# Maxima of three causal attentions: masking the diagonal blocks in SBUF in place of with products

## The chip, the cores and the metric

The kernel runs on one core of one Trainium2 chip. The core has TensorE (PE in the profile: matrix products, results go to the accumulation memory PSUM), VectorE (DVE), ScalarE (ACT), GpSimd (POOL) and SyncE (SP, which here issues DMAs). Each engine takes its own instructions in the order in which they were written; between engines, instructions wait for semaphores. The metric is the device time of one execution in microseconds, smaller is better.

## The reference

A post-norm decoder of two layers on x of 8 batches, 256 tokens and 512 features: in the first layer a differential attention with grouped heads, a long convolution against a context, and a mixture of eight experts with two chosen for each token; in the second a self attention, a cross attention against the context, and an attention with keys and values routed to one head of sixteen. After each of the six, `x = layernorm(x + f(x))`. Three of the six are causal attentions of the form

```
scores = einsum("bhqd,bhkd->bhqk", q, k) * scale
scores = where(causal, scores, very_negative)     # key later than query: hidden
probs  = softmax(scores)                          # exp(score - max over the visible keys), divided by its sum
out    = einsum("bhqk,bhkd->bhqd", probs, v)
```

The softmax subtracts for each query the maximum of its visible scores. This maximum is what the change is about.

## The kernel before

The six parts run one after the other. The three causal attentions share one function, `causal_attention` (L1109): the first runs from about 20 to 470 us of the span, the second from about 1203 to 1541, the third from about 1941 to 2265. Between them stand the convolution and the experts (to 1203) and the cross attention (1541 to 1941).

A **unit** is one batch and four heads. The first attention has 8 units for each of 8 batches, 64 in all (it has 32 heads of scores); the second and third have 4 for each batch, 32 each. Units are numbered `u`; `upb` is the number for each batch. In each unit the 256 tokens make two blocks of 128 queries and two of 128 keys, and since keys later than the query are hidden, three score blocks count: (first queries, first keys) and (second, second), which lie on the diagonal and are half hidden, and (second, first), which is visible as a whole.

What a unit does is spread over `upb + 1` units of the loop (L1357):

- `maxima(u)` (L1154): scores with queries on the partitions. TensorE writes for four heads `s` the three blocks `j` into `ps_q`, a PSUM tile of four banks, one bank for each head. First come four products of `ident_b` and `hide_b` (L1161), which write 0 for visible and -1e30 for hidden pairs into both diagonal blocks; then 12 score products (L1171), each in a 32-row strip of the array, which add to them. VectorE takes the negated maxima of all three blocks with one reduction (L1178) into `neg`.
- After the last unit of a batch, `split(n)` (L1186) joins the two blocks of the second queries and splits the maxima into three bf16 terms (seven small VectorE instructions, L1189 to L1196), and `turn(n)` (L1199) transposes them on TensorE (L1204) and ScalarE copies them out as `negT` (L1212).
- `weights(u)` (L1214), one batch later: scores again, now with keys on the partitions (L1225), with the maxima added by small products (L1234), into `ps_k`; then ScalarE's exp into `pT` (L1242), GpSimd's select that zeroes the hidden half of the diagonal blocks (L1243), and, save in the last batch, a GpSimd add (L1253) that joins two blocks for the row sums.
- `products(u)` (L1255), one unit after that, called by `sums` (L1345): values (L1268), which need the select, and row sums by a matrix of ones (L1278), which need the add, into the PSUM tile `ps_pv`; VectorE's reciprocal of the sums (L1286) and the product with it (L1292, in the first attention L390 and, for the second of a pair of heads, L393 with a GpSimd add L394).

`ps_q` and `ps_k` share one buffer: `maxima(u)` can't begin before the exp of the weights before it, and the weights of a unit can't begin before its maxima are read. `ps_pv` has one buffer too; three more, of the tag `mm`, are for everything else.

The engines' order within the attentions is the order in which the code is written (`manual_schedule`). The loop writes, for each unit: `maxima`, at a batch's end `split`, `sums`, then "mid" events, a short portion of **fill**, `weights`, at a batch's end `turn`, the rest of the fill, "end" events. Fill is other TensorE work cut into steps: projections for the next group of tokens (L205), transposes (L217), output products of finished batches (L205), with its readers on ScalarE or VectorE. When an output tile is complete, VectorE adds the residual (L234) and takes mean and variance (L168, L169), GpSimd computes the reciprocal root (L163, L164), and VectorE normalises one unit later (L177). These GpSimd instructions are written where the fill ended, so they can stand ahead of the unit's select L1243. The first attention also has a GpSimd power for each finished tile of a batch (L469), written as an "end" event.

Of the kernel before, what the change touches and what calls it, by code (L numbers as in the profile page):

```python
# [16 lines left out]
F32 = mybir.dt.float32  # L17
BF16 = mybir.dt.bfloat16
AF = mybir.ActivationFunctionType
ALU = mybir.AluOpType  # L20
AX = mybir.AxisListType
PSUM = bass.MemoryType.PSUM

P = 128
# [7 lines left out]
FAR = 1.0e30  # L32
# [17 lines left out]
def decoder_kernel(ctx: ExitStack, tc: tile.TileContext, a: dict, out: bass.AP):  # L50
    nc = tc.nc
# [4 lines left out]
    const = ctx.enter_context(tc.tile_pool(name="const", bufs=1))  # L56
# [10 lines left out]
    def load_x(tiles):  # L67
# [8 lines left out]
    ident_b = const.tile([P, P], BF16, tag="ident_b", name="ident_b")  # L76
    nc.vector.tensor_copy(ident_b, ident)
    hide_b = const.tile([P, P], BF16, tag="hide_b", name="hide_b")
    nc.gpsimd.memset(hide_b, 0.0)
    nc.gpsimd.affine_select(  # L80
        out=hide_b,
        in_=hide_b,
        compare_op=ALU.is_ge,
        fill=-FAR,
        base=0,
        pattern=[[-1, P]],
        channel_multiplier=1,
    )

# [3 lines left out]
    nc.gpsimd.memset(ones_v, 1.0)  # L93

    mask = const.tile([P, 2 * P], F32, tag="mask", name="mask")
    nc.gpsimd.memset(mask, 0.0)
    nc.gpsimd.affine_select(
        out=mask[:, P:],
        in_=mask[:, P:],
        compare_op=ALU.is_ge,  # L100
        fill=FAR,
        base=0,
        pattern=[[-1, P]],
        channel_multiplier=1,
    )
    neg_half = const.tile([P, H1], F32, tag="neg_half", name="neg_half")
# [1002 lines left out]
    def causal_attention(name, prepare, finish, upb=KB, gather=None):  # L1109
# [9 lines left out]


        engines = {
            mybir.EngineType.PE,
# [4 lines left out]
        with ExitStack() as st:  # L1127
# [26 lines left out]
            def maxima(u):  # L1154
                g, b, c = unit(u)
                q, k, _ = groups[g]
                ps = ps_sc.tile([P, 4, D], F32, tag="sc", name="ps_q")
                block = ps[:, :, : 3 * P].rearrange("p s (j k) -> p s j k", j=3)

                for s in range(4):  # L1160
                    nc.tensor.matmul(  # L1161
                        block[:, s, 0:3:2, :],
                        lhsT=ident_b,
                        rhs=hide_b.unsqueeze(1).broadcast_to([P, 2, P]),
                        start=True,
                        stop=False,
                    )
                for j, (i, keys) in enumerate(((0, 0), (1, 0), (1, 1))):
                    for s in range(4):
                        rows = slice(32 * s, 32 * s + 32)  # L1170
                        nc.tensor.matmul(  # L1171
                            block[:, s, j, :],
                            lhsT=q(rows, c, b * S + i * P, P),
                            rhs=k(rows, c, b * S + keys * P, P),
                            start=False,
                            stop=(j == 2),
                        )
                nc.vector.tensor_reduce(  # L1178
                    neg[(u // upb) % 2][:, :, :, c].rearrange("p j s -> p s j"),
                    block,  # L1180
                    AX.X,
                    ALU.max,
                    negate=True,
                )
# [171 lines left out]
            left = 0.0  # L1356
            for u in range(units + lag + 2):  # L1357
# [6 lines left out]
                if u >= units:  # L1364
# [7 lines left out]
                    continue  # L1372
                maxima(u)
                if u % upb == upb - 1:
                    split(u // upb)
                sums(u)
                happen("mid")
# [6 lines left out]
                if u >= upb:  # L1384
                    weights(u - upb)
                if u % upb == upb - 1:
                    turn(u // upb)
                left = fill(left + rate - short)
                happen("end")
# [464 lines left out]
```

## Time and profile before

| | |
|---|---|
| median of 3 runs | 2280.09 us (2278.44 to 2285.2) |
| the profiled execution's own time | 2277.43 us |
| its span, from first to last instruction | 2275.7 us |
| granted TensorE clock, mean | 0.971 of full speed |
| TensorE busy | 2110.2 us |
| VectorE busy | 1245.9 us |
| GpSimd busy | 679.2 us |
| ScalarE busy | 415.9 us |
| window 83 to 473 us (first attention): PE, DVE, ACT, POOL busy | 355.5, 248.0, 116.3, 190.7 of 390 us |
| window 1203 to 1541 us (second) | 327.9, 178.6, 78.8, 105.6 of 338 us |
| window 1941 to 2265 us (third) | 308.1, 219.5, 66.3, 80.8 of 324 us |

In the lines of a profile "L1178" is a line of the kernel, "neg<-ps_q" what is written and read, "x128" how many. In the groups of part 5 the numbers after the bar are the busy time in us, the mean of one in ns, and the idle time of the engine just before them with what ended most of it. In a timeline the columns are start and duration in us, engine, line, operation, operands and how many are merged; square brackets give the idle time of that engine before it and what released it. In the list of waits they are the total in us, the number of times and the longest. PE is busy time of pipelined products, so its share says little of how close it is to its peak. "PEld" is the loading of weights, which overlaps.

### The profile page before, as it was taken

How to read it: one execution, taken by the hardware profiler on the slowest of the kernel's cores; microseconds unless marked ns; L12 is line 12 of the kernel's file. 1: busy time of each engine (PE TensorE's matmuls, PEld its weight loads, DVE VectorE, ACT ScalarE, POOL GpSimd, SP SyncE). 2: the span in 40 equal slices, each digit the busy share in tenths (PEclk: the TensorE clock that was granted, in tenths of full speed). 3: DMA queues.
4: the chain of work that ended last, by engine and by line, in shares of the span. 5: the costliest groups of instructions: out<-in, count | busy, mean ns of one | idle time of the engine just before them, and what ended most of it. 6: DMA issues, size and time to landing. Idle time of an engine off the chain costs nothing. (4 is left out here: it accounts for less than half of the span.)

```text
span 2275.7 us, 36145 instructions
## 1 busy us (share of the span) xinstructions
PE 2110.2 (93%) x15416; PEld 1236.4 (54%) x15416; DVE 1245.9 (55%) x1923; ACT 415.9 (18%) x595; POOL 679.2 (30%) x780
## 2 busy tenths in 40 slices
PE   7799989888999997999969999997999999999996
PEld 4455555544445455555534454555877875555543
DVE  3566666666889874122234556456343332566767
ACT  1223233330001002211111222221101101122212
POOL 0345544555555833000021334224000000022323
PEclk9899999998999999999989999999999999999998
DMA  7899702403313225123140102002000000000000
GB/s 236 303 384 384 267 2 66 115 1 109 136 44 136 80 92 181 61 81 119 56 158 19 47 29 75 1 1 94 29 19 28 28 10 1 1 11 10 15 15 29
DMA packets 110032, 197.60 MB, mean 87 GB/s; under 512 B 7088, under 2 KB 30768, under 8 KB 109872
## 3 DMA queue, kind: packets, MB, share of 16 engines
q1 hardware_dynamic: 104752, 178.49, 22.7%
q0 software_dynamic: 5120, 16.78, 2.2%
q8 instruction: 124, 2.03, 0.4%
q14 instruction: 36, 0.29, 0.0%
HBM read 93.54 MB, written 112.20 MB: 90 GB/s over the span
## 5 line engine op out<-in xcount | busy, mean ns | idle before, releaser
L1178 DVE TENSOR_REDUCE neg<-ps_q 128x12 f32<-128x1536 f32 x128 | 224.8, 1756 | 340.0 <-PE ps_q L1171 339.3
L1243 POOL TENSOR_SCALAR_AFFINE_SELECT pT<-pT 128x1024 f32<-128x1024 f32 x128 | 140.1, 1095 | 509.6 <-ACT pT L1242 439.7
L194 PE MATMUL ps_y<-kv,wt 128*128 128x512 f32 x640 | 282.5, 600 | 4.4 <-POOL kv L531 3.7
L1242 ACT ACTIVATE pT<-ps_k 128x1536 f32<-128x1536 f32 x128 | 185.6, 1450 | 537.3 <-PE ps_k L1234 506.3
L1286 DVE RECIPROCAL rsum<-ps_pv 128x256 f32<-128x256 f32 x128 | 224.0, 1750 | 42.9 <-PE ps_pv L1278 41.8
L194 PEld LDWEIGHTS ps_y<-kv,wt 128*128 128x128 f32 x640 | 120.8, 192 | 154.5 <-issue 135.2
L1253 POOL TENSOR_TENSOR pT<-pT 128x512 f32<-128x512 f32 x112 | 142.3, 1270 | 9.3
L163 POOL TENSOR_SCALAR rstd<-bn_mv 128x1 f32<-128x1 f32 x80 | 16.5, 206 | 359.5 <-DVE bn_mv L169 355.5
L205 PE MATMUL ps_f<-xT,w_l1a 128*128 128x512 f32 x256 | 120.7, 616 | 3.0 <-ACT xT L218 3.0
L205 PE MATMUL ps_t<-w_l1f,xT 128*128 128x512 f32 x256 | 120.1, 607 | 0.3 <-DVE sel L1671 0.3
L1089 POOL DMA_INDIRECT w_l1x<-ys,slots x32 | 32.7, 1022 | 279.0 <-DMA ys<-y_m 271.1
L1004 PE MATMUL po_m<-dn,hT 128*128 (+1 forms) x216 | 103.3, 616 | 12.0 <-ACT hT L997 10.5
L1278 PE MATMUL ps_pv<-pT,ones_v 128*32 128x256 f32 (+1 forms) x1152 | 86.2, 382 | 13.0 <-POOL pT L1253 10.9
L1161 PEld LDWEIGHTS <-ident_b 128*128 128x128 bf16 x512 | 50.2, 98 | 74.6 <-issue 71.0
L569 DVE TENSOR_REDUCE yc<-z 128x64 f32<-128x512 f32 x128 | 86.0, 673 | 6.2 <-POOL w_l1a L570 5.7
L1161 PE MATMUL ps_q<-hide_b,ident_b 128*128 128x256 bf16 x512 | 77.3, 274 | 9.7 <-ACT pT L1242 8.7
L205 PEld LDWEIGHTS ps_f<-xT,w_l1a 128*128 128x128 f32 x256 | 47.3, 194 | 59.6 <-issue 54.8
L1225 PE MATMUL ps_k<-qT,kz 32*128 32x256 f32 (+1 forms) x1024 | 69.0, 356 | 8.0 <-DVE neg L1178 6.3
L205 PEld LDWEIGHTS ps_t<-w_l1f,xT 128*128 128x128 f32 x256 | 45.5, 189 | 52.2 <-issue 50.5
L986 DVE TENSOR_TENSOR h_b<-h_b,pg 128x352 f32<-128x352 f32 x36 | 18.7, 521 | 100.2 <-ACT h_b L985 100.2
L1268 PE MATMUL ps_pv<-pT,v 128*32 128x256 f32 (+1 forms) x1024 | 56.3, 338 | 18.0 <-POOL pT L1243 16.8
L1225 PE MATMUL ps_k<-qT,kT 32*128 32x256 f32 (+1 forms) x1024 | 68.5, 354 | 3.8 <-ACT pT L1242 2.7
(330 smaller groups left out, 3677.5 us busy)
## 6 DMA issues: line engine op xcount, KB each, us to landing
xs<-zero SPq DMA_DIRECT2D x8, 4352.0 KB
ys<-zero SPq DMA_DIRECT2D x8, 4352.0 KB
filters<-in_L_xattn_k SPq DMA_DIRECT2D x4, 2560.0 KB
first_h<-xs SPq DMA_DIRECT2D x36, 256.0 KB
ys<-y_m SPq DMA_DIRECT2D x36, 256.0 KB
gu<-in_L_ffn_gate_up_proj SPq DMA_DIRECT2D x3, 2816.0 KB
wt<-filters SPq DMA_DIRECT2D x32, 256.0 KB
x<-in_x SPq DMA_DIRECT2D x16, 256.0 KB
```

Of the source, the lines that this page charges most:

```text
L194: nc.tensor.matmul(ps, lhsT=lhsT(k), rhs=rhs(k), start=(k == 0), stop=(k == n - 1))
L205: nc.tensor.matmul(ps[0], lhsT=lhsT(k), rhs=rhs(k), start=(k == 0), stop=(k == KB - 1))
L569: nc.vector.tensor_reduce(yc[:, lb], z, AX.X, ALU.add)
L1004: nc.tensor.matmul(po, lhsT=hT[:m, i, :], rhs=dn[i][:m, bass.ds(e, 1), :], start=(i == 0), stop=(i == len(FCH) - 1),)
L1161: nc.tensor.matmul(block[:, s, 0:3:2, :], lhsT=ident_b, rhs=hide_b.unsqueeze(1).broadcast_to([P, 2, P]), start=True, stop=False,)
L1178: nc.vector.tensor_reduce(neg[(u // upb) % 2][:, :, :, c].rearrange("p j s -> p s j"), block, AX.X, ALU.max, negate=True,)
L1225: nc.tensor.matmul(block[:, s, at, :], lhsT=k(rows, c, b * S + j * P, P), rhs=q(rows, c, b * S + j * P, P * (2 - j)), start=True, stop=False,)
L1242: nc.scalar.activation(p[:, 0:3].rearrange("p j s q -> p s j q"), block, AF.Exp)
L1243: nc.gpsimd.affine_select(out=p[:, 0:2].rearrange("p j s q -> p (j s) q"), in_=p[:, 0:2].rearrange("p j s q -> p (j s) q"), compare_op=ALU ...
L1253: nc.gpsimd.tensor_tensor(p[:, 3], p[:, 1], p[:, 2], ALU.add)
L1278: nc.tensor.matmul(ps[32 * s : 32 * s + 32, 1, j * P :], lhsT=ones_v, rhs=p[:, 1, s, :] if j else first[:, :, s, :], start=(j == 0), stop= ...
L1286: nc.vector.reciprocal(r, ps[:, 1, :])
```

## The change

The four mask products go, and with them `hide_b`. The score products no longer add to anything. Of the three blocks, the visible one is reduced by VectorE from PSUM as before, alone. The two diagonal blocks of the four heads (1024 elements on each partition) are copied by ScalarE into a new SBUF tile `diag` (two buffers); GpSimd's select writes -1e30 over the hidden keys in place; VectorE takes their maxima from SBUF with a second reduction. `maxima` returns this second reduction as a function, and the loop calls it after `sums`.

The order of the loop changes with it. `sums(u)` now comes ahead of `split`, with the second reduction between. `turn` of a batch no longer follows the weights of its last unit but the `maxima` of the next unit, ahead of that unit's `sums`; only the last batch's `turn` stays in its own unit, after the rest of the fill. A constant `mask`, which nothing reads, goes too.

```diff
--- before.py
+++ after.py
@@ -75,34 +75,11 @@
 
     ident_b = const.tile([P, P], BF16, tag="ident_b", name="ident_b")
     nc.vector.tensor_copy(ident_b, ident)
-    hide_b = const.tile([P, P], BF16, tag="hide_b", name="hide_b")
-    nc.gpsimd.memset(hide_b, 0.0)
-    nc.gpsimd.affine_select(
-        out=hide_b,
-        in_=hide_b,
-        compare_op=ALU.is_ge,
-        fill=-FAR,
-        base=0,
-        pattern=[[-1, P]],
-        channel_multiplier=1,
-    )
 
     pick = const.tile([P, 32], F32, tag="pick", name="pick")
     nc.vector.tensor_reduce(pick, ident.rearrange("p (s j) -> p j s", s=4), AX.X, ALU.add)
     ones_v = const.tile([P, 32], F32, tag="ones_v", name="ones_v")
     nc.gpsimd.memset(ones_v, 1.0)
-
-    mask = const.tile([P, 2 * P], F32, tag="mask", name="mask")
-    nc.gpsimd.memset(mask, 0.0)
-    nc.gpsimd.affine_select(
-        out=mask[:, P:],
-        in_=mask[:, P:],
-        compare_op=ALU.is_ge,
-        fill=FAR,
-        base=0,
-        pattern=[[-1, P]],
-        channel_multiplier=1,
-    )
     neg_half = const.tile([P, H1], F32, tag="neg_half", name="neg_half")
     nc.gpsimd.memset(neg_half, -0.5)
 
@@ -1118,6 +1095,7 @@
 
 
 
+
         engines = {
             mybir.EngineType.PE,
             mybir.EngineType.DVE,
@@ -1156,15 +1134,6 @@
                 q, k, _ = groups[g]
                 ps = ps_sc.tile([P, 4, D], F32, tag="sc", name="ps_q")
                 block = ps[:, :, : 3 * P].rearrange("p s (j k) -> p s j k", j=3)
-
-                for s in range(4):
-                    nc.tensor.matmul(
-                        block[:, s, 0:3:2, :],
-                        lhsT=ident_b,
-                        rhs=hide_b.unsqueeze(1).broadcast_to([P, 2, P]),
-                        start=True,
-                        stop=False,
-                    )
                 for j, (i, keys) in enumerate(((0, 0), (1, 0), (1, 1))):
                     for s in range(4):
                         rows = slice(32 * s, 32 * s + 32)
@@ -1172,15 +1141,26 @@
                             block[:, s, j, :],
                             lhsT=q(rows, c, b * S + i * P, P),
                             rhs=k(rows, c, b * S + keys * P, P),
-                            start=False,
-                            stop=(j == 2),
+                            start=True,
+                            stop=True,
                         )
-                nc.vector.tensor_reduce(
-                    neg[(u // upb) % 2][:, :, :, c].rearrange("p j s -> p s j"),
-                    block,
-                    AX.X,
-                    ALU.max,
-                    negate=True,
+
+                d = work.tile([P, 4, 2, P], F32, tag="diag", name="diag")
+                nc.scalar.copy(d, block[:, :, 0:3:2, :])
+                dst = neg[u // upb % 2][:, :, :, c]
+                nc.vector.tensor_reduce(dst[:, 1], block[:, :, 1, :], AX.X, ALU.max, negate=True)
+                rows = d.rearrange("p s j k -> p (s j) k")
+                nc.gpsimd.affine_select(
+                    out=rows,
+                    in_=rows,
+                    compare_op=ALU.is_ge,
+                    fill=-FAR,
+                    base=0,
+                    pattern=[[0, 8], [-1, P]],
+                    channel_multiplier=1,
+                )
+                return lambda: nc.vector.tensor_reduce(
+                    dst[:, 0:3:2].rearrange("p j s -> p s j"), d, AX.X, ALU.max, negate=True
                 )
 
             def split(n):
@@ -1370,10 +1350,13 @@
                     left = fill(left + rate)
                     happen("end")
                     continue
-                maxima(u)
+                diagonal = maxima(u)
+                if u and u % upb == 0:
+                    turn(u // upb - 1)
+                sums(u)
+                diagonal()
                 if u % upb == upb - 1:
                     split(u // upb)
-                sums(u)
                 happen("mid")
                 if u % upg == upb and u // upg + 1 < NG:
                     per_group = begin(u // upg + 1)
@@ -1383,9 +1366,9 @@
                 left = fill(left + short)
                 if u >= upb:
                     weights(u - upb)
-                if u % upb == upb - 1:
+                left = fill(left + rate - short)
+                if u == units - 1:
                     turn(u // upb)
-                left = fill(left + rate - short)
                 happen("end")
             while after or current or events:
                 now[0] += 1
```

## The prediction

> **What bounds the kernel now.** I read the page first. Part 1 names TensorE; part 5 gives the size of what the diff touches: 512 mask products and 128 reductions, one per unit.
>
> ```profile
> PE 2110.2 (93%) x15416; PEld 1236.4 (54%) x15416; DVE 1245.9 (55%) x1923; ACT 415.9 (18%) x595; POOL 679.2 (30%) x780
> ...
> L1178 DVE TENSOR_REDUCE neg<-ps_q 128x12 f32<-128x1536 f32 x128 | 224.8, 1756 | 340.0 <-PE ps_q L1171 339.3
> ...
> L1161 PE MATMUL ps_q<-hide_b,ident_b 128*128 128x256 bf16 x512 | 77.3, 274 | 9.7 <-ACT pT L1242 8.7
> ```
>
> 93% invites the answer "TensorE is the bound, so save its products". The waits say where it isn't:
>
> ```profile
> PEld ps_k L1225 <- DVE neg L1178: 30.1, 36, 1.3
> ...
> PEld ps_pv L1278 <- POOL pT L1253: 27.1, 53, 0.8
> ```
>
> In 53 units the ones products wait for GpSimd. So I went through the timeline unit by unit, counting units from 0 in the order of L1178 (0 to 63 in the first attention, 64 to 95 in the second, 96 to 127 in the third). One unit of the first attention:
>
> ```profile
> 171.47 0.60 PE L1161 MATMUL ps_q<-hide_b,ident_b 128*128 128x256 bf16 x4
> ...
> 172.00 0.95 PE L1171 MATMUL ps_q<-kz,qT 32*128 32x128 f32 x24
> ...
> 172.91 1.27 POOL L1253 TENSOR_TENSOR pT<-pT 128x512 f32<-128x512 f32 x1
> 173.02 1.76 DVE L1178 TENSOR_REDUCE neg<-ps_q 128x12 f32<-128x1536 f32 x1 [1.15 <-PE ps_q L1171]
> 174.23 0.64 PE L1278 MATMUL ps_pv<-pT,ones_v 128*32 128x256 f32 x8 [0.49 <-POOL pT L1253]
> ...
> 174.94 1.76 DVE L1286 RECIPROCAL rsum<-ps_pv 128x256 f32<-128x256 f32 x1 [0.16 <-PE ps_pv L1278]
> ...
> 177.13 0.68 DVE L234 TENSOR_TENSOR res<-ps_o,x 128x512 f32<-128x512 f32 x1
> ...
> 178.57 0.18 DVE L169 BATCH_NORM_AGGREGATE bn_mv<-bn_st 128x2 f32<-128x6 f32 x1
> ...
> 179.12 0.57 POOL L164 TENSOR_TENSOR rstd<-rstd,neg_half 128x1 f32<-128x1 f32 x1
> 179.65 1.10 POOL L1243 TENSOR_SCALAR_AFFINE_SELECT pT<-pT 128x1024 f32<-128x1024 f32 x1
> ```
>
> Two things. The loop weights, exp, select, add, ones, weights closes in 6.86 us where nothing else intervenes (ones products of units 28 and 29 at 203.39 and 210.25), and the mask products aren't in it. And the select at 179.65 was due at 178.6, when the exp ended; it stood behind L164, which stood behind DVE's statistics, and DVE had been busy since 173.02 with 0.16 us of gap. A unit of the second attention is different: GpSimd is early, and TensorE runs through.
>
> ```profile
> 1432.75 0.60 PE L1161 MATMUL ps_q<-hide_b,ident_b 128*128 128x256 bf16 x4
> ...
> 1432.96 1.27 POOL L1253 TENSOR_TENSOR pT<-pT 128x512 f32<-128x512 f32 x1
> 1433.28 0.95 PE L1171 MATMUL ps_q<-kT,qT 32*128 32x128 f32 x24
> ...
> 1434.83 0.40 PE L1278 MATMUL ps_pv<-pT,ones_v 128*32 128x256 f32 x4
> ```
>
> DVE's own timeline shows that units 0 to 11 can't gain at all: all queues meet at a DMA at 78.2 us.
>
> ```profile
> 78.21 1.29 DVE L301 TENSOR_SCALAR w_l<-w_l,lnw 128x2048 f32<-128x2048 f32 x1 [7.75 <-DMA lv<-in_L_attn_lambda_k]
> ```
>
> **What the Trainium skill says.** (1) PSUM — Partial Sum Buffer, "PSUM bank collisions raise a hardware error": no two engines may touch one bank of a quadrant at once, two reads included, and the software has to order them. Each head's three blocks lie in one bank, so VectorE's reduction of the middle block must follow ScalarE's copy of the outer two. No row of before shows such a pair. (2) VectorE: DVE Perf Modes, "The perf-mode tier table": `tensor_reduce` has the 1x mode alone. The trace agrees: 673 ns at 512 elements (L569, from SBUF), 1756 ns at 1536. (3) TensorEngine Tiling (Array Packing), "Key Properties": a change of tiling mode drains TensorE. Measured: matmul L205 to L1225, which splits rows, is 0.52 us start to start, against 0.43 to a full-array matmul.
>
> **The change part by part.**
>
> *Mask products gone.* Now: L205 to mask 0.43 us, mask to first score 0.53, together 0.96. After: 0.52, as L205 to L1225. Saved 0.43 us of TensorE per unit, where TensorE is what ends last. Units 12 to 63: in 39 of 52 the ones products start 0.05 us after the GpSimd add, so 0; in 10 the slack is above 0.43; in three it is 0.14, 0.15 and 0.34; in five of the 39 the weights then wait for the reduction (start 1.88 us after the last score) and come 0.28 earlier. 10 x 0.43 + 0.63 + 5 x 0.28 = 6.3 us. Second attention: 11 of 32 units have their scores held by ScalarE's evacuation of q or k (mask to score 0.85), one waits for GpSimd, four are spoilt below; 16 x 0.43 = 6.9. Third: 4 held by evacuation, 6 by GpSimd, 3 spoilt; 19 x 0.43 = 8.2. Gain 21.4 us. The four constants less at the start (GpSimd, 0.3 us each) lie ahead of a 7 us DMA wait of L285: nothing.
>
> *Copy and first reduction.* ScalarE copy of 1024 elements: 585 ns at 512 (L139), 1450 at 1536 (L1242), so 1.02 us. Reduction of 512: 0.69 (673 and L1558's 692). One after the other, with 0.1 for the waits: PSUM is free 1.82 us after the last score, now 1.83. No gain for the weights behind it. If both read at once it is 1.09. ScalarE is free at that moment in all but six units, and the next exp is 2 us or more away: the copy costs nothing there. Without that cover it would cost 1.02.
>
> *GpSimd select.* As L1243, 1.1 us, from 1.1 to 2.2 us after the scores; the next select there is due at 5 or later. Hidden, except behind the 2.9 us powers L469, issued two in a row: units 19 and 35 have GpSimd full until the select, 1.1 each; unit 51 0.84; units 26, 44, 59 together 0.5. Loss 3.5.
>
> *Diagonal reduction.* 1024 elements from SBUF: 1.2 us from the two rows above. Bounds: 0.65, if it ran at two elements a cycle, and 1.5, if it shares SBUF with GpSimd as the longest select (1382 ns against 1091) does; I take 1.2. It stands behind the reciprocal and its products. As the reciprocal starts no earlier than now (PSUM part over at 1.82), all that follows on DVE in the unit is 1.2 us later: L234, L168, L169, and through L163/L164 GpSimd's select. That costs where this chain already makes the select late. First attention: units 24, 31, 40 at 1.1, unit 63 1.5 with its end: 4.8. Second: units 72, 74, 75, 80 to 83, their slack deducted: 1.2 + 0.4 + 1.1 + 0.4 + 0.2 + 0.8 + 0.8 = 4.9. Third: units 105, 109, 113, 118, 121 at 1.0 to 1.2, unit 126 0.2: 6.0. Loss 15.7.
>
> *Split and turn.* The seven small split instructions (1.4 us) now follow the reciprocal, which starts 1.4 us earlier for it: what comes after is 1.2 later, as above. The turn goes one unit on, between scores and values. Queued behind it are the products. In the first attention the split ends about 6.7 us after the scores and the turn is reached at 6.7 to 6.8: no stall, but no slack. In the others units are 8 to 11 us long. At a stage's last unit the turn follows diagonal and split directly, and the exp waits: 0.8 for the second, 1.65 for the third. Loss 2.4.
>
> Sum: 21.4 gained, 3.5 + 15.7 + 2.4 = 21.6 lost. On the profiled execution's 2277.43 us (span 2275.7) that is 2277.6; the median of the runs lies 2.7 higher. I forecast 2279.
>
> **The rivals.**
>
> *Faster, 2266.* The DVE delay doesn't reach TensorE: the diagonal reduction costs 0.65, or both engines read PSUM at once, so that reciprocals start at 1.31 instead of 1.74. Losses fall to about a third, 7 us: 21.4 - 7 = 14. For it: GpSimd and ScalarE have the room, and the slack of most units is above 0.6. Against: the 1x mode and the bank rule.
>
> *Slower, 2292.* The turn stalls. TensorE takes its work in order, so a turn that waits for the split holds values, ones and weights of that unit. Its slack at the seven batch ends of the first attention is 0 to 0.1 us, so it decides as soon as a split ends later than 6.8 us after its scores. At 1.0 us each, 7; with the diagonal at its upper price, 0.3 x 15 = 4.5 more: about 12. For it: in the old order the split ends at 3.26 and the turn is reached at 3.9 (unit 15), 0.7 of room that is now gone. Against: other DVE work of the unit stands behind the split.
>
> *TensorE is simply the bound,* 128 x 0.43 = 55 us, so 2225: against it stand the 53 waits for GpSimd and the DMA at 78 us. I give it 2 in 100, within faster.
>
> **How the numbers follow.** No gain within 0.3% (6.8 us, about what a measurement of this kernel can tell from no change): 0.37, its own range 2272 to 2286. Faster: 0.35. Slower: 0.28. The range 2262 to 2296 leaves out the far ends of both, about 2 in 10, and holds the bounds of diagonal and reading order.
>
> **What would show it.** Score products 0.52 us after the preceding matmul; the first reduction starting at the copy's end, about 1.1 us after the last score; the diagonal reduction near 1.2 us; the sum of DVE up by some 18 us (0.69 + 1.2 - 1.76 = 0.13 a unit), ScalarE by 130, GpSimd by 140; the waits of ones products for the GpSimd add longer in total, not shorter. The prediction is wrong if the select after the exp is no later than before in units 105, 109, 113 and 121, or if the turns wait for the split in the first attention.

## The result, and the profile after

The kernel after takes 2307.49 us (median of 4 runs, 2304.89 to 2313.47) against 2280.44 us of the kernel before beside it (2278.44 to 2285.2). The ratio is 1.0119, with a 95% interval of 1.0093 to 1.0145: slower by 27 us, outside the predicted range of 2262 to 2296.

From the page of the kernel after: the engines' sums (part 1), and of the groups (part 5) those that stand where L1178 and L1161 stood.

```profile
PE 2078.3 (90%) x14904; PEld 1200.5 (52%) x14904; DVE 1282.2 (56%) x2051; ACT 545.9 (24%) x723; POOL 814.5 (35%) x904
...
L1151 DVE TENSOR_REDUCE neg<-ps_q 128x4 f32<-128x512 f32 x128 | 88.4, 691 | 311.7 <-ACT diag L1149 311.6
...
L1153 POOL TENSOR_SCALAR_AFFINE_SELECT diag<-diag 128x1024 f32<-128x1024 f32 x128 | 140.0, 1094 | 186.3 <-ACT diag L1149 186.2
...
L1162 DVE TENSOR_REDUCE neg<-diag 128x8 f32<-128x1024 f32 x128 | 155.3, 1213 | 26.1 <-POOL diag L1153 26.0
```

The single operations came as priced: the first reduction 691 ns (predicted 0.69 us), and always behind ScalarE's copy; the select 1094 ns (1.1 us); the diagonal reduction 1213 ns (1.2 us). ScalarE rose by 130 us and GpSimd by 135, as predicted, VectorE by 36 in place of 18. TensorE has 32 us less of busy time and the kernel is 27 us longer. What TensorE waits for has changed (list of waits of the kernel after: us in total, times, longest):

```profile
PE ps_pv L1248 <- POOL pT L1223: 47.3, 34, 11.5
PE ps_n L1184 <- DVE terms L1173: 28.4, 11, 4.8
PE ps_pv L1258 <- POOL pT L1233: 22.4, 47, 0.6
```

The lines are values for the select, turn for the split, and row sums for the add. The same three of the kernel before, in the order of its own list:

```profile
PE ps_pv L1268 <- POOL pT L1243: 23.5, 12, 9.4
...
PE ps_pv L1278 <- POOL pT L1253: 10.9, 28, 0.5
...
PE ps_n L1204 <- DVE terms L1193: 6.1, 5, 3.3
```

So row sums do wait longer in total, as the prediction said. The wait of the turn, from 6.1 to 28.4 us, is what it called its own refutation: the turns wait for the split.

Where the 27 us are, from the start of the first score product of one unit to that of another, in the two profiled executions. "Lost clock" is half of the time for which the records show a TensorE clock of 0.50:

| stretch | before, us | after, us | difference | lost clock before, after |
|---|---|---|---|---|
| start to unit 12 | 89.5 | 88.7 | -0.8 | |
| units 12 to 63 (first attention) | 369.8 | 396.7 | **+26.9** | 3.4, **29.0** |
| unit 63 to 64 (with convolution and experts) | 745.2 | 743.7 | -1.5 | |
| units 64 to 95 (second) | 326.4 | 325.9 | -0.5 | 0, 1.7 |
| unit 95 to 96 (with cross attention) | 411.3 | 412.0 | +0.7 | |
| units 96 to 127 (third) | 293.8 | 291.8 | -2.0 | 5.1, 6.8 |
| unit 127 to the end | 39.7 | 44.3 | +4.6 | |

Nearly the whole loss lies in units 12 to 63. The second and third attention end 2 us later than before when their last unit is counted, where the prediction had them 1.8 us earlier. The end of unit 15 and unit 16 show what happens in the first (timeline of the kernel after):

```profile
114.75 1.09 POOL L1223 TENSOR_SCALAR_AFFINE_SELECT pT<-pT 128x1024 f32<-128x1024 f32 x1 [3.38 <-ACT pT L1222]
114.92 1.00 DVE L1176 TENSOR_TENSOR less<-neg,terms 128x64 f32<-128x64 f32 x1
...
115.92 1.26 POOL L1233 TENSOR_TENSOR pT<-pT 128x512 f32<-128x512 f32 x1
115.95 1.29 DVE L1173 CAST terms<-less 128x64 bf16<-128x64 f32 x1
117.14 1.09 POOL L1153 TENSOR_SCALAR_AFFINE_SELECT diag<-diag 128x1024 f32<-128x1024 f32 x1
117.27 1.03 DVE L1176 TENSOR_TENSOR less<-less,terms 128x64 f32<-128x64 f32 x1
...
118.59 0.41 PE L1184 MATMUL ps_n<-ident_b,terms 128*32 128x128 bf16 x8 [2.91 <-DVE terms L1173]
...
118.77 1.50 PE L1248 MATMUL ps_pv<-pT,v 128*32 128x256 f32 x16
...
121.06 2.08 PE L182 MATMUL ps_f<-xT,w_l 128*128 128x512 f32 x2
```

The same instructions of the split in the kernel before, in the same unit:

```profile
111.97 0.23 DVE L1196 TENSOR_TENSOR less<-neg,terms 128x64 f32<-128x64 f32 x1
...
112.46 0.23 DVE L1196 TENSOR_TENSOR less<-less,terms 128x64 f32<-128x64 f32 x1
```

Three things are to be seen. An instruction of the split that took 0.19 to 0.23 us takes 1.00 to 1.29, and each ends just after the GpSimd instruction that was running ends: 115.92 after 115.84, 117.24 after 117.18, 118.30 after 118.23. The split then takes 4.1 us (114.46 to 118.54) instead of 1.4. The turn waits 2.91 us for it on TensorE, and values and row sums, whose inputs are there from 115.84 and 117.18 on, stand behind the turn. And after the stall TensorE is slow: the 16 values products take 1.50 us instead of 0.86, the two projections 2.08 instead of 1.13. Unit 16 takes 11.71 us; before it took 6.87.

**Theory: the held split.** GpSimd's new work and its old work now run while the split runs, hold it, and the turn, placed ahead of the products, carries the delay to TensorE, which then also runs at half clock for a while. **Rivals:** the norm chain (the diagonal reduction delays residual and statistics, these the roots and the select), GpSimd too full (its select of the diagonal delays powers, selects and adds), and, for the slow products, a clock that falls for another reason than the stall.

### The profile page after: what moved, and what is told of

Its sections match the earlier page's. It is cut to its first block, busy times and chain, and to the rows that moved or that the text cites. A ratio compares the mean times of both kernels' runs of the same rounds, so it can differ in the third digit from the quotient of the medians.

```text
span 2303.1 us, 35720 instructions
## 1 busy us (share of the span) xinstructions
PE 2078.3 (90%) x14904; PEld 1200.5 (52%) x14904; DVE 1282.2 (56%) x2051; ACT 545.9 (24%) x723; POOL 814.5 (35%) x904
## 5 line engine op out<-in xcount | busy, mean ns | idle before, releaser
L1151 DVE TENSOR_REDUCE neg<-ps_q 128x4 f32<-128x512 f32 x128 | 88.4, 691 | 311.7 <-ACT diag L1149 311.6
L1153 POOL TENSOR_SCALAR_AFFINE_SELECT diag<-diag 128x1024 f32<-128x1024 f32 x128 | 140.0, 1094 | 186.3 <-ACT diag L1149 186.2
L1149 ACT COPY diag<-ps_q 128x1024 f32<-128x1024 f32 x128 | 129.7, 1013 | 188.8 <-PE ps_q L1140 171.0
L1162 DVE TENSOR_REDUCE neg<-diag 128x8 f32<-128x1024 f32 x128 | 155.3, 1213 | 26.1 <-POOL diag L1153 26.0
L140 POOL TENSOR_SCALAR rstd<-bn_mv 128x1 f32<-128x1 f32 x80 | 16.9, 211 | 322.1 <-DVE bn_mv L146 317.8
L1205 PE MATMUL ps_k<-qT,kz 32*128 32x256 f32 (+1 forms) x1024 | 75.4, 382 | 4.5 <-DVE neg L1151 4.2
L1140 PEld LDWEIGHTS ps_q<-kT,qT 32*128 32x128 f32 x1536 | 49.2, 188 | 57.3 <-issue 31.6
L1140 PEld LDWEIGHTS ps_q<-kz,qT 32*128 32x128 f32 x1536 | 49.9, 190 | 55.7 <-ACT pT L1222 35.1
```

Source lines behind the costliest of these rows:

```text
L1140: nc.tensor.matmul(block[:, s, j, :], lhsT=q(rows, c, b * S + i * P, P), rhs=k(rows, c, b * S + keys * P, P), start=True, stop=True,)
L1149: nc.scalar.copy(d, block[:, :, 0:3:2, :])
L1153: nc.gpsimd.affine_select(out=rows, in_=rows, compare_op=ALU.is_ge, fill=-FAR, base=0, pattern=[[0, 8], [-1, P]], channel_multiplier=1,)
L1162: return lambda: nc.vector.tensor_reduce(dst[:, 0:3:2].rearrange("p j s -> p s j"), d, AX.X, ALU.max, negate=True)
L1205: nc.tensor.matmul(block[:, s, at, :], lhsT=k(rows, c, b * S + j * P, P), rhs=q(rows, c, b * S + j * P, P * (2 - j)), start=True, stop=False,)
```

## The experiments

The runs were made on three chips. On one of them the kernel before takes 2263.6 us, on the others 2278.4 and 2278.5, so kernels are compared by their ratio to the kernel before on the same chip; expectations in us are meant on 2280. Units that no edit touches repeat from chip to chip (unit 22 took 6.83 or 6.84 us in all thirteen profiles), and the kernel after once more had 396.8 us from unit 12 to 63 where the first time had 396.7. A stretch with other lost clock repeats less well: its third attention had 294.8 us in place of 291.8, with 3.4 us more of lost clock. "Kernel 2" is the kernel of experiment 2, and so on.

**1. The turn behind the products.**

```diff
                 diagonal = maxima(u)
-                if u and u % upb == 0:
-                    turn(u // upb - 1)
                 sums(u)
+                if u and u % upb == 0:
+                    turn(u // upb - 1)
                 diagonal()
```

> The kernel after, with one call moved: a batch's turn stands behind the products of the next unit instead of ahead of them. Theory 'held split' (the split's small VectorE instructions are held by GpSimd, end late, and the turn that waits for them stops values and row sums): the products no longer stand behind that wait, so the total of TensorE's waits at L1184 falls from 28.4 us to under 12, and the time falls by 10 to 18 us, to 2289 to 2297. Rival 'norm chain' (the diagonal reduction delays residual and statistics on VectorE, these the roots on GpSimd, these the select after the exp): nothing on that chain moves, 2304 to 2310. Rival 'GpSimd too full' (the select of the diagonal delays powers, select and add): 2304 to 2310 as well.

Ratio 1.0121 (1.0100 to 1.0141), as the kernel after. The waits at the turn fell to 17.8 us only (3.2 of them in units 12 to 63, where there had been 12.6), and the expectation is missed; taken alone, this run speaks for the rivals. Unit 16 fell from 11.71 to 7.88 us, but units 25, 32, 36 and 41 stayed as long as they were, and so did the lost clock of units 12 to 63, 25.6 us. That stretch took 390.4 us, 6.3 less. So the turn's place alone is worth little while the split itself is still late. The kernel after, once more, beside others:

> The kernel after once more, beside the three that follow, on the chip that they run on. If moving the turn alone changed nothing (the ratio 1.0121 of that kernel against 1.0119 of this one), it lies at 1.012 of the kernel before here too; if it is over 1.014, moving the turn was a gain.

1.0128 (1.0105 to 1.0152), under the bound set: moving the turn alone made no difference that these runs can tell.

**2. The split without a second SBUF input.** The minimum of the two blocks, the copies and the subtractions become reductions over one or two neighbouring elements; the values are the same.

```diff
-                nc.vector.tensor_tensor(rest[:, 1], rest[:, 1], rest[:, 2], ALU.min)
+                reduced(pair[:, 0, 0], whole[:, 0].unsqueeze(3))
+                reduced(pair[:, 0, 1], whole[:, 1:3].rearrange("p j s c -> p s c j"), ALU.min)
...
-                    nc.vector.tensor_copy(t, rest)
+                    reduced(t, flat(pair[:, 0]))
...
-                        nc.vector.tensor_tensor(less, rest, t, ALU.subtract)
+                        reduced(pair[:, 1]..., t.unsqueeze(3), negate=True)
+                        reduced(after[:, 0]..., pair.rearrange("p t j s c -> p (j s c) t"), ALU.add)
```

> The kernel after, with the split's arithmetic done by VectorE reductions over one or two elements, which have a single SBUF input, in place of tensor_tensor and tensor_copy; same values, two or three more small instructions, same place in the order. Theory 'held split': no instruction of the split takes more than 0.25 us whatever GpSimd does (now 0.95 to 1.29 where they meet), the split takes under 2.2 us, TensorE's waits at the turn fall from 28.4 us to under 12, and the time falls by 8 to 18 us, to 2289 to 2299. Rivals 'norm chain' and 'GpSimd too full': 2304 to 2311. If the small instructions are long for a reason other than their operands (a wait for the result before them, say), they stay at about 1 us here too.

Ratio 1.0075 (1.0055 to 1.0095): 10 us of the 27 are back, in the expected 8 to 18. The split behind unit 15 takes 2.2 us in place of 4.1. Units 12 to 63 took 380.3 us in place of 396.7, with 15.4 us of lost clock in place of 29.0. One line of the split, in the kernel after and in this one (number, then shortest, median and longest duration in ns); first after:

```profile
L1176 DVE TENSOR_TENSOR less<-less,terms x24: 191/208/1098, 51.5 to 2269.8; 128x32 f32<-128x32 f32 x16, 128x64 f32<-128x64 f32 x8
```

and here, for the subtraction as a reduction:

```profile
L1170 DVE TENSOR_REDUCE pair<-pair x48: 219/222/291, 51.0 to 2245.0; 128x32 f32<-128x64 f32 x32, 128x64 f32<-128x128 f32 x16
```

No reduction takes over 291 ns, whatever GpSimd does. The Trainium skill says why, in SBUF — State Buffer, "Who interferes with whom": VectorE and GpSimd share a pair of ports, which one of them holds for a whole instruction while the other waits; a VectorE instruction with two SBUF inputs needs it against a GpSimd instruction that reads SBUF, copies and casts can need it, and a `tensor_reduce` on this chip never does. The trace agrees with each part: L1176 (two inputs) 1.0 us, the cast L1173 up to 1289 ns, and the diagonal reduction L1162 at a median of 1211 ns both alone and with GpSimd running. The prediction did not use that page. Unit 16 is 7.11 us here. TensorE's waits at the turn fell from 12.6 to 5.6 us in units 12 to 63, but to 20.4 only over the whole kernel, where under 12 were expected: the rest, 3.0 us ahead of unit 12 and 2.9 to 3.8 at each of the three ends of an attention, is as large as in the kernel after. At an attention's end the turn stands directly behind diagonal and split.

**3. The masking alone, in the old order.**

```diff
                 diagonal = maxima(u)
-                if u and u % upb == 0:
-                    turn(u // upb - 1)
-                sums(u)
                 diagonal()
                 if u % upb == upb - 1:
                     split(u // upb)
+                sums(u)
```

(with the turn behind the weights of its own unit)

> The kernel after with the old order of the loop: diagonal reduction and split directly behind the maxima and ahead of the products, the turn behind the weights of its own unit. This is the change of the masking alone. Now VectorE waits for GpSimd's select before the reciprocal, which starts about 3.4 us after the last score instead of 1.8. Theory 'held split': waits at the turn vanish (under 8 us in total), but everything on VectorE is 1.5 us later than in the kernel after, so 2295 to 2310. If the new order as such is what costs, 2280 to 2290. If the new order is a gain that the masking eats, over 2312.

Ratio 1.0504 (1.0476 to 1.0533), by the medians 112 us slower than before on its chip. The last of the named readings holds by its bound (over 2312 on the scale of 2280): the new order is a gain that the masking needs. Why so much, from the timeline of unit 15 of this kernel:

```profile
113.72 1.27 POOL L1233 TENSOR_TENSOR pT<-pT 128x512 f32<-128x512 f32 x1
114.94 1.09 POOL L1153 TENSOR_SCALAR_AFFINE_SELECT diag<-diag 128x1024 f32<-128x1024 f32 x1
...
116.06 1.22 DVE L1162 TENSOR_REDUCE neg<-diag 128x8 f32<-128x1024 f32 x1 [2.35 <-POOL diag L1153]
...
118.63 1.75 DVE L1266 RECIPROCAL rsum<-ps_pv 128x256 f32<-128x256 f32 x1
```

The select of the diagonal stands on GpSimd behind the add, VectorE stands 2.35 us and waits for it (162.7 us in all), and the reciprocal starts 6.7 us after the last score (111.91). What follows the reciprocal, the second head's GpSimd add L371 among it, is late, and that add stands ahead of the next select. The expectation had only the 1.1 us of an idle GpSimd in mind. Lost clock of units 12 to 63: 44.4 us.

**4. What the products themselves are worth.** Into the kernel before.

```diff
-                for s in range(4):
-                    nc.tensor.matmul(
-                        block[:, s, 0:3:2, :],
-                        lhsT=ident_b,
-                        rhs=hide_b.unsqueeze(1).broadcast_to([P, 2, P]),
...
-                            start=False,
-                            stop=(j == 2),
+                            start=True,
+                            stop=True,
```

> The kernel before without its mask products and with nothing in their place: the maxima are taken over the hidden keys of the diagonal blocks too (the masking of the maxima is left out). It measures what the removal of the products is worth by itself. The prediction's first term says 21 us, 2259 (2252 to 2266). If TensorE is simply the bound, 55 us, 2225. If GpSimd's add and VectorE's reductions set the pace everywhere, under 7 us, 2274 to 2281.

Ratio 0.9915 (0.9890 to 0.9940): 19 us faster, against 21 predicted. By stretches: second attention 326.4 to 316.9 us, third 293.8 to 285.2, its end 39.7 to 37.7, but the first 369.8 to 371.8, a loss of 2.0 where the prediction had a gain of 6.3. Its lost clock went from 3.4 to 11.9 us. The five units with half clock here (25, 32, 41, 52, 58) are together 6.1 us longer than in the kernel before, the other 46 together 4.1 us shorter. So most of the saving is there, and the half clock takes more than it, although the only edit was to take work from TensorE.

**5. Work in the gaps of every unit.** Four products as large as the mask products, between a unit's values and row sums, in the first attention: into kernel 4, and into kernel 2.

```diff
+                if gather and not late:
+                    for _ in range(4):
+                        nc.tensor.matmul(
+                            ps[:, 1, :],
+                            lhsT=ident_b,
+                            rhs=ident_b.unsqueeze(1).broadcast_to([P, 2, P]),
+                            start=True,
+                            stop=True,
+                        )
```

> The kernel without mask products and with the hidden keys included in the maxima (the masking of the maxima is left out), and, in the first attention, four products of the size of the mask products (identity by identity, results overwritten) between a unit's values and its row sums, where TensorE mostly waits for GpSimd's add. Theory 'half clock' (a stretch of 3.4 us in which TensorE is busy less than about half is followed by 3.4, 6.8 or more us at half clock, and the work taken from TensorE in the first attention makes such stretches): lost clock of units 12 to 63 falls from 11.9 us to under 6 (before: 3.4), and although work is added the time is 0 to 7 us below that of the same kernel without them (ratio 0.9915), so 0.988 to 0.9915. Rival 'work is work': the clock has nothing to do with it, four products cost up to 0.43 us in each of some 13 units that TensorE bounds, 3 to 6 us more: 0.9928 to 0.994.

0.9942 (0.9925 to 0.9959). The lost clock fell in the theory's direction, from 11.9 to 6.8 us (under 6 expected), but units 12 to 63 took 371.6 us, hardly less than 371.8, and the time went the rival's way. Unit by unit both are at work: the five units that had half clock in kernel 4 took 6.2 us less together, the other 46 took 6.0 more, of which 3.3 in units 50, 51, 57 and 60, where half clock now fell.

> The kernel with the split by reductions, and in the first attention the four products between values and row sums. Theory 'half clock': lost clock of units 12 to 63 falls from 15.4 us to under 9 and the time by 2 to 8 us, ratio 1.004 to 1.0067. Rival 'work is work': 1.008 to 1.010.

1.0108 (1.0077 to 1.0140), with the same 15.4 us of lost clock, where under 9 were expected: the rival again. Work in every unit costs at least what it saves. These two leave the clock theory open, since they change both; the next one puts the work only where TensorE stands.

**6. Work in the stall alone.** Sixteen products ahead of the turn of the kernel after.

```diff
                 ps = pools.tile([P, 2, P], F32, tag="mm", name="ps_n")
+                for _ in range(16 if gather and 0 < n < units // upb - 1 else 0):
+                    nc.tensor.matmul(
+                        ps,
+                        lhsT=ident_b,
+                        rhs=ident_b.unsqueeze(1).broadcast_to([P, 2, P]),
+                        start=True,
+                        stop=True,
+                    )
```

> The kernel after, with 16 more products (identity by identity, 1.7 us in all, results overwritten) ahead of each turn of the first attention but the first, so inside the time in which TensorE waits for the split (2.91, 2.69, 1.69, 2.72 and 2.61 us in units 16, 24, 40, 48 and 56; none in unit 32). The wait is as long as before, only TensorE is busy in it. Theory 'half clock' (the stall costs twice: the wait itself, and the half clock that follows a stretch of 3.4 us with little work): the half clock from 117.6 to 124.4 us disappears and unit 16 falls from 11.7 to about 10 us, and unit 24 from 10.3 to about 8.7, although work was added; unit 32 rises by about 1.7; units 12 to 63 together 0 to 10 us shorter than 396.7. Rival (the slow products after the stall have another cause): units 16 and 24 as long as before, unit 32 longer, units 12 to 63 398 us or more.

Ratio 1.0087 (1.0069 to 1.0104), below the kernel after with 1.0128 and 1.0119, with more work in it. Unit 16 fell from 11.71 to 8.96 us, units 12 to 63 from 396.7 to 386.5, the lost clock from 29.0 to 13.7. Busy times in the window of the wait and the two after it, first in the kernel after (the columns are stretch, its length, busy us of PE, PEld, DVE, ACT and POOL, granted clock, share of the DMA engines, GB/s):

```profile
114.20:117.60 3.40, 0.95 (x24) 0.76 (x24) 3.23 (x6) 1.49 (x2) 2.77 (x3) 1.00 1.04 385
117.60:124.40 6.80, 5.81 (x50) 2.65 (x54) 4.66 (x6) 0.97 (x2) 1.35 (x2) 0.50 1.03 383
```

and here, where unit 16 begins 1.05 us later:

```profile
115.20:118.60 3.40, 2.80 (x40) 2.25 (x40) 3.23 (x6) 1.53 (x2) 2.73 (x3) 1.00 1.04 386
118.60:125.40 6.80, 5.19 (x82) 2.73 (x84) 4.92 (x6) 3.14 (x4) 2.05 (x3) 1.00 1.03 383
```

The split is as long as in the kernel after and the turn starts as late (2.92 us after the scores, 2.91 in the kernel after), but TensorE worked 2.80 us of the 3.40 instead of 0.95, and its clock stayed at 1.00. The added products, the turn and the values behind it:

```profile
116.65 1.92 PE L1183 MATMUL ps_n<-ident_b 128*128 128x256 bf16 x16
...
119.64 0.29 PE L1192 MATMUL ps_n<-ident_b,terms 128*32 128x128 bf16 x8 [1.06 <-DVE terms L1173]
...
119.76 0.82 PE L1256 MATMUL ps_pv<-pT,v 128*32 128x256 f32 x16
```

The values products take 0.82 us where they took 1.50. That settles the rival on the clock for unit 16: the stall brought the half clock. Unit 24 fell to 9.75 us only, where 8.7 were expected, and unit 32, expected 1.7 longer, fell from 12.46 to 10.42, with its half clock gone. What half clock costs shows in unit 25: it took 8.46 to 8.70 us in the five profiles in which its clock stayed full, and 11.68 to 12.84 in the seven in which it had half clock for 6.8 us or more. Unit 20 is not touched by the edit and lost its stretch of half clock too; where the windows of the clock fall against a unit differs from one execution to the next, so single stretches away from the edit prove nothing.

**7. The diagonal reduction at the end of the unit.** Into kernel 2, save for a batch's last unit.

```diff
                 sums(u)
-                diagonal()
-                if u % upb == upb - 1:
-                    split(u // upb)
+                last = u % upb == upb - 1
+                if last:
+                    diagonal()
+                    split(u // upb)
...
                 left = fill(left + rate - short)
+                if not last:
+                    diagonal()
```

> The kernel with the split by reductions, and with the diagonal reduction of all but a batch's last unit moved from behind the products to the end of the unit, behind residual and statistics on VectorE. Theory 'norm chain' (the diagonal reduction ahead of residual and statistics makes GpSimd's roots and so its select late; in the second and third attention this eats the gain of the missing products): the second and third attention together come 8 to 16 us down, the first by 0 to 5, and the ratio falls from 1.0075 to 0.999 to 1.004. If only the split and the half clock cost, it stays at 1.006 to 1.009.

Ratio 1.0024 (1.0013 to 1.0035) after 1.0075, in the expected band. In the profiles the fall is smaller than the ratio's and smaller than expected for the second and third attention: 1.8 us in units 12 to 63, 2.3 in the second, 2.8 in the end of the third, none in units 96 to 127, which had 3.4 us more of lost clock. What the chain looks like in the kernel after, at unit 109 (timeline):

```profile
2087.61 1.21 DVE L1162 TENSOR_REDUCE neg<-diag 128x8 f32<-128x1024 f32 x1
...
2088.73 0.68 DVE L211 TENSOR_TENSOR res<-ps_y,x 128x512 f32<-128x512 f32 x1
...
2091.70 0.18 DVE L146 BATCH_NORM_AGGREGATE bn_mv<-bn_st 128x2 f32<-128x6 f32 x1
...
2092.25 0.55 POOL L141 TENSOR_TENSOR rstd<-rstd,neg_half 128x1 f32<-128x1 f32 x1
...
2092.76 1.10 POOL L1223 TENSOR_SCALAR_AFFINE_SELECT pT<-pT 128x1024 f32<-128x1024 f32 x1
...
2093.91 0.86 PE L1248 MATMUL ps_pv<-pT,v_r 128*32 128x256 f32 x16 [1.56 <-POOL pT L1223]
```

and in kernel 7:

```profile
2080.97 1.10 POOL L1237 TENSOR_SCALAR_AFFINE_SELECT pT<-pT 128x1024 f32<-128x1024 f32 x1
...
2082.11 0.86 PE L1262 MATMUL ps_pv<-pT,v_r 128*32 128x256 f32 x16 [0.42 <-POOL pT L1237]
```

In the kernel after the exp ended at 2089.42, and its select starts 3.34 us later, behind the roots (L140, L141); in the kernel before it is 2.18 us, in kernel 7 2.21. The values stand 1.56 us for it, and 0.42 in kernel 7. Units 106, 110 and 114 take 10.90, 11.86 and 11.76 us in kernel 2, 9.80, 10.74 and 10.64 in kernel 7, and 9.97, 10.70 and 10.66 in the kernel before. So the norm chain is real, with 1.1 us in each of these.

**8. Without GpSimd's select of the diagonal.** Into kernel 7; the masking of the maxima is left out, copy and second reduction stay.

```diff
-                nc.gpsimd.affine_select(
-                    out=rows,
-                    in_=rows,
...
```

> The kernel with the split by reductions and the late diagonal reduction, without GpSimd's select of the diagonal copy (the masking of the maxima is left out; copy and second reduction stay). It measures what GpSimd's new 1.1 us for each unit costs. The prediction's term: 3.5 us, behind the powers (units 19, 35, 51), so 1.0024 becomes 1.000 to 1.0015, and unit 20 and unit 36 fall back to the 7.3 us of the kernel before from 9.0 and 10.7. If the load on GpSimd is what eats the gain in general, below 0.997. If it costs nothing, 1.002 to 1.004.

Ratio 0.9994 (0.9986 to 1.0003) after 1.0024: 7 us, twice the term of 3.5, with intervals that leave some 4 to 10. Unit 36 fell from 10.65 to 7.97 us, unit 20 from 9.01 to 8.02; neither came back to 7.3. In the kernel after, unit 20 shows it: the power L446 ends at 147.80, then come the diagonal's select (1.11 us), and then the exp's; the values waited 2.12 us.

**9. Diagonal and turn both late.** Into kernel 7.

```diff
                 diagonal = maxima(u)
-                if u and u % upb == 0:
-                    turn(u // upb - 1)
                 sums(u)
+                if u and u % upb == 0:
+                    turn(u // upb - 1)
```

> The kernel with the split by reductions and the late diagonal reduction, and the turn behind the products of the next unit. TensorE's waits at the turn in the first attention (6.2 us in six places) vanish; with them 3 to 7 us, so 1.0024 becomes 0.9995 to 1.001. If the turn's place no longer matters once the split isn't held, 1.002 to 1.003.

Ratio 0.9984 (0.9972 to 0.9997), a little better than expected. The six waits at the turn in units 16 to 56, 6.2 us in kernel 7, are gone. Units 12 to 63 took 370.1 us with 3.4 us of lost clock; the kernel before has 369.8 and 3.4. The turn's place, worth nothing measurable in experiment 1, brings 8.4 us in the profile here, where the split is quick; the time fell by 9 us (0.0040 of 2278). With all three places mended the new masking is a shade faster than the kernel before (0.16%), where it was 1.2% slower.

This version, with the masking of the change in full, thus beats both kernels, and so does kernel 4 with 0.9915 (and kernel 4 with the added products of experiment 5). Kernel 4 subtracts a maximum over visible and hidden keys, which the quotient of the softmax cancels as long as no hidden score lies so far above all visible ones that their exponentials vanish; whether that holds is a matter of the data.

## Why the prediction was wrong

Its sum leads to 2277.6 us for the profiled execution and, with the 2.7 us of the median, to 2280.3; why it says 2279 it doesn't tell, and nothing hangs on it. By its own steps:

- **Mask products gone, 21.4 us: right in the sum, not in its parts.** Kernel 4 gained 19 us: 20 in the second and third attention, where 15.1 were predicted, and in the first a loss of 2.0 instead of 6.3 gained. There the units at full clock gained 4.1 us and the five with half clock lost 6.1, a term that the sum didn't have. That the total came so close is in part luck.
- **Copy and first reduction: right in most units.** PSUM is read 1.81 us after the last score in unit 15 (copy to 1.08, reduction 1.11 to 1.81), and within 1.86 us in 96 of 128 units; predicted 1.82. In the first unit of a batch the held split delays the reduction too: it ends at 3.45 us in unit 16 and at 4.32 in unit 48. No run takes ScalarE's copy out, so that it costs nothing isn't shown.
- **GpSimd select, 3.5 us: right place, size 7.** It costs behind the powers as said; a values product that waits over 2 us can then meet half clock as well (in kernel 7 unit 36 did, with 10.65 us against 7.97 without the select; unit 20 didn't).
- **Diagonal reduction, 15.7 us: confirmed in kind.** After the exp the select comes later than before by 1.39, 1.16, 1.11 and 1.10 us in units 105, 109, 113 and 121, which the prediction put at 1.0 to 1.2, and three units behind them are 1.1 us shorter with the reduction out of the way. Moving the reduction of all but the batch-ending units away was worth 0.0051, 12 us by the medians, with intervals that leave some 6 to 17; the profile shows 7.
- **Split and turn, 2.4 us: the step that failed.** It said that "in the first attention the split ends about 6.7 us after the scores and the turn is reached at 6.7 to 6.8: no stall, but no slack". It took the split's 1.4 us from the old order, where it ran with GpSimd idle (unit 15). In unit 15 it began 5.8 us after the last score and ended at 9.9. The turns of units 16, 24, 40, 48 and 56 wait 2.91, 2.69, 1.69, 2.72 and 2.61 us, 12.6 together, and the stall in unit 16 halves TensorE's clock for 6.8 us. Kernel 2, which only unlocks the split, takes 16.4 us off units 12 to 63. TensorE's busy time in that stretch falls by 11.8 us with the same products (338.4 to 326.6): they ran at half clock less often. Another 8.4 us come with the turn behind the products (experiment 9). At the ends of the attentions the turn waits 2.8, 3.1 and 4.8 us, where the sum had nothing, 0.8 and 1.65; the third shows in the stretch from unit 127 to the end, 4.6 us longer.

In the profiles of units 12 to 63 the three edits in turn take off 16.4 (split), 1.8 (diagonal late) and 8.4 us (turn late), 26.6 of the 26.9 lost. These are single profiles, and the parts depend on the order in which they are taken: the turn alone, taken first, took 6.3 us off this stretch in its profile and made no measurable difference in time.

The rival "slower, 2292" named the right mechanism and place, with 1.0 us for each of seven batch ends. The waits were 1.7 to 2.9 us in five of them, and the half clock came on top. With 12.6 for the waits and the 11.8 of slow products in units 12 to 63 in place of its 7 it would have said 2292 - 7 + 24.4 = 2309, an estimate after the fact from these numbers. It was not given that size because the durations of the split were taken as fixed, whatever ran beside it. A price for sharing SBUF with GpSimd stands in the prediction only on the diagonal reduction (its bound of 1.5 us), where the runs show none. "Faster" is out: the diagonal reduction is 1213 ns and the two PSUM reads are serial. "TensorE is simply the bound" is out too: without the products the time falls by 19 us, not by 55.

## What to carry to other kernels

A step that is moved keeps its instructions but not its durations: look at what the engine that shares its SBUF ports does at the new place, and give small vector instructions there a reduction's form, if a chain hangs on them (one SBUF input alone isn't enough: casts, which have one, were held too). A stall of an engine whose clock falls when it has little to do can be paid twice, and work taken away from it can bring such a fall: read the granted clock by stretches before and after, not its mean. An in-order queue should reach a late step after what is ready, not ahead of it; but mend the late step first, or moving it shows nothing.

## What the runs showed of the hardware that was not expected

- **VectorE held by GpSimd.** In the kernel after, 23 instructions of the split, 18 with two SBUF inputs and 5 casts from f32 to bf16, began while a GpSimd instruction ran that had over 0.3 us to go. All 23 took 0.65 to 1.29 us in place of 0.17 to 0.23, and ended 0.02 to 0.09 us after that instruction. Reductions of the same data never took over 0.30.
- **Half clock after slack.** All stretches of low clock in the attentions are at 0.50 and last 3.4 us or multiples (6.8, 10.2, 13.7). The Trainium skill, TensorE: Matmul & The Clock Gate, "Part 1: The HAM clock gate (the "warmup" mystery)", describes a free-running window of about 3.4 us and half rate after an idle one. Here the window needn't be idle. Counted on that grid in units 12 to 63 of all thirteen profiles, of 75 windows at full clock in which TensorE was busy for less than half, 68 were followed by half clock; of 1252 with half or more, 13.
- **Less work, lower clock.** Without its mask products (0.60 us of busy time in each unit) and with nothing in their place, the first attention lost 11.9 us of clock instead of 3.4. Its five stretches of half clock follow 3.4 us with TensorE 45 to 51% busy. Two of these places (units 32 and 58) had half clock before, too; at the other three the emptiest windows of the kernel before were 64, 55 and 68% busy. In those five units the first attention loses more than the other 46 gain by the missing products.
